# Selective-scan units whose product with B runs on GpSimd and whose decay lies in PSUM

## The chip, the cores and the metric

The kernel runs on one core of one Trainium2 chip. The metric is the device time of one execution in microseconds. The engines are called as in the profile: PE is TensorE, DVE is VectorE, ACT is ScalarE, POOL is GpSimd and SP is SyncE, which here issues nearly all DMAs.

## What is computed

Four layers work on an activation of 4 images x 1024 positions x 256 channels, in float32. The parts that matter here are the two selective scans, in layer 0 (512 inner channels, 64 states each) and in layer 3 (512 inner channels, 16 states each). In short:

```python
def step(h, inp):                                   # layer 0; layer 3 is alike
    xt, dtt, Bt, Ct = inp
    dA = jnp.exp(dtt[:, :, None] * A)               # the decay
    h = dA * h + (dtt * xt)[:, :, None] * Bt[:, None, :]
    y = jnp.einsum('bdn,bn->bd', h, Ct)
    return (h, y)
```

Around them layer 0 has a layer norm, a projection, a depthwise convolution, GELU and an output projection. Layer 1 is a residual block with a grouped convolution. Layer 2 is masked attention and a mixture of eight experts. Layer 3 has projections, the scan, a gate and another mixture of eight experts.

## The kernel before, in words

**Units.** A scan of one image is cut into units. One unit is a tile of 128 rows (channel times state) by 1024 steps of time: two channels of layer 0 or eight channels of layer 3. There are four images, so layer 0 has 4 x 256 units and layer 3 has 4 x 64, 1280 in all, numbered in the order of `SCANS`: (0,0), (0,1), (3,0), (0,2), (3,1), (0,3), (3,2), (3,3), where a pair is layer and image. Layer 3's units are thus 512 to 575, 832 to 895 and 1152 to 1279.

**What one unit takes.** `scans` writes the units as a software pipeline. In iteration k, in this order:

- `load(k + 4)`: SP loads the rows of dt, each repeated over the states, from DRAM into a tile `dA` (five buffers). That is two DMAs of 256 KB in layer 0 and eight of 64 KB in layer 3.
- `first(k + 1)`: two bf16 matmuls on PE spread dt times u over the states, from three bf16 parts, into a PSUM tile `ps_rep` (tag "x", two buffers).
- `decay(k + 2)`: ACT takes the exponential of the loaded tile in place, with a column of A as the scale.
- the mul: DVE multiplies `ps_rep` by the rows of B in PSUM. Then, after a `yield`, DVE runs `tensor_tensor_scan` with the decay from `dA` and the input from `ps_rep` into `h` (five buffers), and POOL multiplies `h` by the rows of C.
- `pair(k - 2)`, in every second iteration: PE sums two units over the states into `ps_y`, eight matmul records in the trace (four per unit). When a group of channels is full, ACT copies it out and SP stores it.

The scan of the next unit and the mul of the next unit follow on DVE in this order, so DVE alternates mul, scan, mul, scan. A `ps_rep` buffer comes free when the scan two units earlier ends.

**Side work.** Everything else inside `run` (the fronts of layer 0, then `middle(b)`, which holds layer 0's end, layers 1 and 2 and the front of layer 3, then `last(b)`) is a chain of Python generators. At each `yield` of `scans`, `run` may advance them by up to two steps. A planner, `Metered`, adds up a modelled cost for each engine; side work is admitted only as long as no engine's modelled clock is ahead of DVE's ("vector"), and no clock may lag DVE's by over 4 us:

```python
if max(clock.values()) > clock["vector"] + LEAD or self.advance() is None:
```

The order so found is the order of the instructions (the scheduler is set to manual). Where a scan needs something that side work hasn't produced, `need` advances the side work at once, with no scan between. For the last group of units, image 3 of layer 3, this happens between the scans of units 1210 and 1211. `last(3)` runs after all scans.

**The front's `steps`** compute dt and dt times u, store dt to DRAM, split dt times u in three bf16 parts and store these. The tile `x0`, 128 x 2048 float32 in SBUF, holds image 0 and is used by the first front only.

Most instructions are recorded through `Metered`'s helper, so the profile shows them at line 122; they are told apart by their tiles.

Of the kernel before, what the change touches and what calls it, by code (L numbers as in the profile page):

```python
# [16 lines left out]
P = 128  # L17
NB = 4
L = 1024
# [19 lines left out]
SORTS = 2  # L39
AHEAD = 12  # L40
LATEST = 5

LEAD, LAG, TICKS = 0.0, 4.0, 2
# [81 lines left out]
class Hybrid:  # L127
# [182 lines left out]
    def scan_setup(self, stage, psum, name, n):  # L310
# [16 lines left out]
        nc.vector.tensor_scalar(cols, cols, -1.0, None, ALU.mult)  # L327
        spread = pool.tile([3 * 32, 32 // G, P], BF16, name="spread_" + name)
        for s in range(3):
# [15 lines left out]
    def scans(self, mp, psum):  # L345
# [7 lines left out]
        nc = self.nc  # L353
        units = []
        for scan in SCANS:
            G = P // self.states[scan[0]]
# [2 lines left out]
                for d in range(DC) for c in range(2) for i in range(32 // G) for j in range(2)  # L359
            ]  # L360
        chunks, rows, waiting = {}, {}, []
        state = {}
        y = None

# [26 lines left out]
        def chunks_ahead(k):  # L391

            if k + AHEAD < len(units) and units[k + AHEAD][2:] == (0, 0, 0):
                waiting.append(k + AHEAD)
            while waiting:
                scan, d = units[waiting[0]][:2]
                if waiting[0] - k > LATEST and ("parts", *scan, d) not in self.ready:
                    break
                chunk(waiting.pop(0))

        def load(k):
            if k >= len(units):
                return
            scan, d, c, i, j = units[k]
            n = self.states[scan[0]]
            G = P // n
            a = mp.tile([P, L], F32, tag="dA", name="dA", bufs=5)
            for g in range(G):
                r = 64 * c + 32 * j + G * i + g
                nc.sync.dma_start(  # L410
                    a[g * n : (g + 1) * n, :],
                    self.mem["dt", *scan, d][r : r + 1, :].to_broadcast([n, L]),
                )
            state[k] = a

        def decay(k):
            if k >= len(units):
                return
            scan, d, c, i, j = units[k]
            G = P // self.states[scan[0]]  # L420
            col = (d * P + 64 * c + 32 * j) // G + i
            nc.scalar.activation(
                state[k], state[k], AF.Exp, scale=self.tables[scan[0]][0][:, col : col + 1]
            )

        def first(k):
            if k >= len(units):
                return
            scan, d, c, i, j = units[k]
            spread = self.tables[scan[0]][1]  # L430
            G = P // self.states[scan[0]]
            ps = psum.tile([P, L], F32, tag="x", name="ps_rep", bufs=2)
            for g in range(2):
                cols = slice(g * 512, (g + 1) * 512)
                nc.tensor.matmul(
                    ps[:, cols], lhsT=spread[:, i, :], rhs=chunks[scan, d][:, 2 * c + j, cols],
                    start=True, stop=True,
                )
            state[k] = (state[k], ps)
# [30 lines left out]
        for k in range(4):  # L470
            load(k)
        decay(0)
        decay(1)
        first(0)
        for k in range(len(units) + 4):
            chunks_ahead(k)
            load(k + 4)
            first(k + 1)
            decay(k + 2)
            if k < len(units):  # L480
                a, inp = state.pop(k)
                B, Cm = rows[units[k][0]]
                nc.vector.tensor_tensor(inp, inp, B, ALU.mult)
            yield
            if k < len(units):
                h = mp.tile([P, L], F32, tag="h", name="h", bufs=5)
                nc.vector.tensor_tensor_scan(h, a, inp, 0.0, ALU.mult, ALU.add)
                nc.gpsimd.tensor_tensor(h, h, Cm, ALU.mult)
                state[k] = h
            if k % 2 == 1 and 2 <= k < len(units) + 2:  # L490
                pair(k - 2)
            yield

    def need(self, scan, d):
# [26 lines left out]
    def run(self):  # L521

        self.done, self.ready = set(), set()
        self.todo, self.stage = list(STAGES), None
        nc, tc = self.nc, self.tc
        with tc.tile_pool(name="scan", bufs=1) as mp, tc.tile_pool(
            name="scps", bufs=1, space=PSUM
        ) as psum, tc.tile_pool(name="sdps", bufs=1, space=PSUM) as side, tc.manual_schedule():
            self.side_psum(side)
            self.mask_work, self.sorted = self.mask_prepare(), False  # L530
            clock = self.clock = dict.fromkeys(Metered.COST, 0.0)
            self.nc = Metered(nc, clock)
            for n, _ in enumerate(self.scans(mp, psum)):
                if n % 2:
                    next(self.mask_work, None)
                now = clock["vector"]
                for e in clock:
                    clock[e] = max(clock[e], now - LAG)
                for _ in range(TICKS):
                    if max(clock.values()) > clock["vector"] + LEAD or self.advance() is None:  # L540
                        break
            while self.advance() is not None:
                pass
            self.nc = nc
        assert not self.todo
# [7 lines left out]
    def steps(self, fp, key, w, src, chunks, bias, u):  # L553


        nc = self.nc
        for d in range(DC):
            self.keep(("dt", *key, d), [P, L])
            self.keep(("parts", *key, d), [3, P, L], BF16)
        got = {}  # L560

# [1194 lines left out]
```

## Time and profile before

| | |
|---|---|
| median of 3 runs | 6912.75 us (6912.15 to 6918.07) |
| the profiled execution | 6914.57 us, span 6912.9 us |
| PE busy | 5388.0 us, 78% |
| DVE busy | 5204.9 us, 75% |
| POOL busy | 3644.9 us, 53% |
| ACT busy | 3440.9 us, 50% |
| DMA queue of SP | 930.53 MB, 51.1% of 16 engines' span |
| granted PE clock, mean | 0.82 |

A row of the page's list of groups gives line, engine, operation, output and input tiles with their shape and count, then the busy time, the mean time of one in ns, and the idle time of the engine just before these instructions, with what ended it. A row of the timeline gives start, duration and engine. Busy shares are averages over stages that have different limits, so the stretches are looked at one by one.

### The profile page before, as it was taken

Reading aid. Unit: us, or ns where it says so; the run is one execution under the profiler, and the core shown is the slowest. Engines: PE = TensorE matmul, PEld = TensorE weight load, DVE = VectorE, ACT = ScalarE, POOL = GpSimd, SP = SyncE. Lnnn points to the kernel's source line nnn. Section 1 sums busy time; section 2 is a strip of 40 time slices with the busy share of each in tenths; the row PEclk is TensorE's granted clock in tenths of the full one; section 3 lists DMA queues with packets and bytes.
Section 4 is the critical chain, followed back from the end, with each engine's and each line's share of the span. In section 5 each row is a group of like instructions: output and inputs, shape, how many; then the busy total and the mean of one; then the engine's idle time right before and its main releaser. Section 6 shows DMA issues by size and latency. Waiting matters only on the chain. (4 is left out here: it accounts for less than half of the span.)

```text
span 6912.9 us, 66308 instructions
## 1 busy us (share of the span) xinstructions
PE 5388.0 (78%) x20516; PEld 2219.1 (32%) x20516; DVE 5204.9 (75%) x4477; ACT 3440.9 (50%) x4145; POOL 3644.9 (53%) x1801
## 2 busy tenths in 40 slices
PE   6558768678797567879689668798698678867979
PEld 3002212222342032234145322243253322523556
DVE  7778988877898986889889867898899840237411
ACT  2426667345476333457568334477386332244411
POOL 0876776755557654555856545557666530035200
PEclk8568768679898577989789779898698889877989
DMA  1556665654466665446656655456666630145321
GB/s 71 147 147 161 176 173 157 183 134 113 119 173 169 157 164 128 116 126 177 184 142 165 174 135 124 121 150 173 168 165 167 162 95 0 49 123 144 95 61 34
DMA packets 394239, 937.47 MB, mean 136 GB/s; under 512 B 83220, under 2 KB 165729, under 8 KB 392225
## 3 DMA queue, kind: packets, MB, share of 16 engines
q1 hardware_dynamic: 391696, 930.53, 51.1%
q8 instruction: 172, 2.82, 0.2%
q0 software_dynamic: 2128, 2.13, 0.2%
q14 instruction: 243, 1.98, 0.1%
HBM read 842.59 MB, written 93.95 MB: 135 GB/s over the span
## 5 line engine op out<-in xcount | busy, mean ns | idle before, releaser
L122 POOL TENSOR_TENSOR h<-h,rows 128x1024 f32<-128x1024 f32 x1280 | 3028.5, 2369 | 2002.5 <-DVE h L122 1620.7
L122 DVE TENSOR_TENSOR_SCAN h<-dA,ps_rep 128x1024 f32<-128x1024 f32 x1280 | 2924.6, 2285 | 209.8 <-issue 89.5
L122 DVE TENSOR_TENSOR ps_rep<-ps_rep,rows 128x1024 f32<-128x1024 f32 x1280 | 1553.3, 1213 | 336.3 <-PE ps_rep L122 313.8
L122 ACT ACTIVATE dA<-dA,A_L_conv_A_log 128x1024 f32<-128x1024 f32 x1024 | 1152.3, 1145 | 693.0 <-DMA dA<-dt 582.1
L122 PE MATMUL ps_rep<-S,spread_L_conv_A_log 96*128 96x512 bf16 x2048 | 755.7, 459 | 751.9 <-DVE h L122 696.0
L122 PE MATMUL ps_y<-h,collect_L_conv_A_log 128*32 128x512 f32 x4096 | 774.0, 750 | 104.3 <-POOL h L122 104.2
L122 ACT ACT_TABLE_LOAD x486 | 623.5, 1283 | 72.4 <-PE ps_h L122 49.9
L122 PEld LDWEIGHTS <-spread_L_conv_A_log 96*128 96x128 bf16 x2048 | 164.3, 103 | 1502.8 <-DVE h L122 1157.5
L122 PE MATMUL ps_h<-xTm,we 128*128 128x512 f32 x1280 | 605.7, 609 | 5.6 <-ACT h_m L122 4.5
L122 PE MATMUL ps_e<-we,h_m 128*128 128x256 f32 x2560 | 589.1, 382 | 6.8 <-ACT h_m L122 6.8
L122 ACT ACTIVATE p<-ps_sc 128x512 f32<-128x512 f32 x512 | 277.9, 594 | 588.7 <-PE ps_sc L122 558.6
L122 PEld LDWEIGHTS ps_e<-we,h_m 128*128 128x128 f32 x2560 | 483.2, 190 | 137.1 <-issue 46.7
L122 ACT ACTIVATE dA<-dA,A_L_attn_A_log 128x1024 f32<-128x1024 f32 x256 | 293.4, 1148 | 460.6 <-DMA dA<-dt 434.6
L122 PE MATMUL ps_at<-p,v 128*32 128x512 f32 x1024 | 361.6, 624 | 61.4 <-ACT p L122 53.3
L122 PE MATMUL ps_rep<-S,spread_L_attn_A_log 96*128 96x512 bf16 x512 | 188.8, 458 | 266.5 <-DVE h L122 220.9
L122 ACT ACTIVATE h_m<-ps_h,cols 128x512 f32<-128x512 f32 x320 | 217.0, 687 | 313.2 <-PE ps_h L122 310.4
L122 DVE SCALAR_TENSOR_TENSOR tb<-ps_e,cw,tb 128x256 f32<-128x256 f32 x448 | 192.6, 473 | 214.4 <-PE ps_e L122 214.4
L122 PEld LDWEIGHTS ps_h<-xTm,we 128*128 128x128 f32 x1280 | 242.5, 194 | 287.0 <-issue 238.7
L122 PE MATMUL ps_sc<-qT,kT 32*128 32x512 f32 x1024 | 301.8, 665 | 0.0
L122 PE MATMUL ps_at<-p,ones 128*32 128x512 f32 x1024 | 278.7, 624 | 0.0
L122 PE MATMUL ps_cv<-pad,diag 128*128 128x512 f32 x576 | 260.4, 593 | 0.0
L122 PEld LDWEIGHTS ps_y<-h,collect_L_conv_A_log 128*32 128x32 f32 x4096 | 101.3, 119 | 488.5 <-POOL h L122 240.3
(360 smaller groups left out, 5454.3 us busy)
## 6 DMA issues: line engine op xcount, KB each, us to landing
dA<-dt SPq DMA_DIRECT2D x2048, 256.0 KB
dA<-dt SPq DMA_DIRECT2D x2048, 64.0 KB
we<-in_L_ffn_W_dram SPq DMA_DIRECT2D x64, 512.0 KB
parts<-parts SPq DMA_DIRECT2D x64, 384.0 KB
S<-parts SPq DMA_DIRECT2D x96, 256.0 KB
dt<-sp_r SPq DMA_DIRECT2D x64, 256.0 KB
y<-yo SPq DMA_DIRECT2D x128, 128.0 KB
y_back<-y SPq DMA_DIRECT2D x64, 256.0 KB
```

The costliest lines, as they stand in the source:

```text
L122: return got(*args, **kw)
```

## The change

For some units, called *own* in the code, the input of the scan is made in another way. `steps` now also stores dt times u as float32 (`dtu`). `choose(k + 6)` decides, with a budget of POOL time that the planner leaves unused (`OWN`, 4.0 us each), whether unit k + 6 is own. If so, SP loads the rows of `dtu`, repeated over the states, into one half of `x0`. Two iterations ahead of the scan POOL multiplies this tile by the rows of B, in place. PE's two matmuls and DVE's mul are left out for this unit. Since the scan's input is then in SBUF, its decay goes to PSUM: the exponential reads the loaded `dA` and writes a tile `ps_dA`, from the same two buffers as `ps_rep`, one iteration later than before. For all units `h` has seven buffers instead of five, and `pair` sums units k - 5 and k - 4 instead of k - 3 and k - 2.

```diff
+OWN, EARLY = 4.0, 6
...
+        def spread(k, what, to):
...
+            for g in range(G):
+                r = 64 * c + 32 * j + G * i + g
+                nc.sync.dma_start(
+                    to[g * n : (g + 1) * n, :],
+                    self.mem[what, *scan, d][r : r + 1, :].to_broadcast([n, L]),
+                )
+
         def load(k):
...
+            state[k] = mp.tile([P, L], F32, tag="dA", name="dA", bufs=5)
+            spread(k, "dt", state[k])
+
+        def choose(k):
+            nonlocal spare
+            spare, self.unused = min(spare + self.unused, 1.5 * OWN), 0.0
+            if k >= len(units) or spare < OWN or units[k][:2] not in chunks:
+                return
+            if len(own) > 1 and k - EARLY <= list(own)[-2]:
+                return
+            spare -= OWN
+            i = 4 * (len(own) % 2)
+            own[k] = self.x0[:, i : i + 4, :].rearrange("p j c -> p (j c)")
+            spread(k, "dtu", own[k])
...
         def decay(k):
...
+            if k in own:
+                nc.gpsimd.tensor_tensor(own[k], own[k], rows[units[k][0]][0], ALU.mult)
+            else:
+                nc.scalar.activation(state[k], state[k], AF.Exp, scale=column(k))
 
         def first(k):
-            if k >= len(units):
+            if k >= len(units) or k in own:
                 return
...
-        for k in range(len(units) + 4):
+        for k in range(len(units) + 6):
             chunks_ahead(k)
+            choose(k + EARLY)
             load(k + 4)
             first(k + 1)
             decay(k + 2)
             if k < len(units):
                 a, inp = state.pop(k)
                 B, Cm = rows[units[k][0]]
-                nc.vector.tensor_tensor(inp, inp, B, ALU.mult)
+                if k not in own:
+                    nc.vector.tensor_tensor(inp, inp, B, ALU.mult)
+            if k + 1 in own:
+                ps = psum.tile([P, L], F32, tag="x", name="ps_dA", bufs=2)
+                nc.scalar.activation(ps, state[k + 1], AF.Exp, scale=column(k + 1))
+                state[k + 1] = ps, own[k + 1]
             yield
             if k < len(units):
-                h = mp.tile([P, L], F32, tag="h", name="h", bufs=5)
+                h = mp.tile([P, L], F32, tag="h", name="h", bufs=7)
                 nc.vector.tensor_tensor_scan(h, a, inp, 0.0, ALU.mult, ALU.add)
                 nc.gpsimd.tensor_tensor(h, h, Cm, ALU.mult)
                 state[k] = h
-            if k % 2 == 1 and 2 <= k < len(units) + 2:
-                pair(k - 2)
+            if k % 2 == 1 and 4 <= k < len(units) + 4:
+                pair(k - 4)
...
                 now = clock["vector"]
+                self.unused += max(0.0, now - LAG - clock["gpsimd"])
...
             self.keep(("dt", *key, d), [P, L])
+            self.keep(("dtu", *key, d), [P, L])
...
             nc.sync.dma_start(self.mem["dt", *key, d][:, g * 512 : (g + 1) * 512], r)
+            nc.sync.dma_start(self.mem["dtu", *key, d][:, g * 512 : (g + 1) * 512], x)
```

More of the change, by code (lines that the diff above doesn't have):

```diff
@@ L361, in scans @@
         chunks, rows, waiting = {}, {}, []
+        own, spare = {}, 0.0
         state = {}
@@ L399, in chunks_ahead @@
                 chunk(waiting.pop(0))
+        def spread(k, what, to):
+            scan, d, c, i, j = units[k]
+            n = self.states[scan[0]]
+            G = P // n
+            for g in range(G):
[4 more added lines that the diff above has]
+                )
         def load(k):
@@ L403, in load, with column @@
                 return
-            scan, d, c, i, j = units[k]
[L405 to L414, printed above, removed]
+            state[k] = mp.tile([P, L], F32, tag="dA", name="dA", bufs=5)
[11 more added lines that the diff above has]
+            spread(k, "dtu", own[k])
+        def column(k):
+            scan, d, c, i, j = units[k]
+            col = (d * P + 64 * c + 32 * j) // (P // self.states[scan[0]]) + i
+            return self.tables[scan[0]][0][:, col : col + 1]
         def decay(k):
@@ L418, in decay @@
                 return
[L419 to L424, printed above, removed]
+            if k in own:
+                nc.gpsimd.tensor_tensor(own[k], own[k], rows[units[k][0]][0], ALU.mult)
+            else:
+                nc.scalar.activation(state[k], state[k], AF.Exp, scale=column(k))
         def first(k):
-            if k >= len(units):
+            if k >= len(units) or k in own:
                 return
@@ L532, in run @@
             self.nc = Metered(nc, clock)
+            self.unused = 0.0
             for n, _ in enumerate(self.scans(mp, psum)):
```

## The prediction

> **What bounds the kernel now.** I read the page's costliest groups first, then where the scans of the 1280 units start in time, then the busy time by stretch, then waits and SP's timeline. A unit is one `tensor_tensor` (mul, with B) and one scan on DVE, one product with C on POOL, one exponential on ACT, two `ps_rep` matmuls and four `ps_y` matmuls on PE. From the page:
>
> ```profile
> L122 POOL TENSOR_TENSOR h<-h,rows 128x1024 f32<-128x1024 f32 x1280 | 3028.5, 2369 | 2002.5 <-DVE h L122 1620.7
> L122 DVE TENSOR_TENSOR_SCAN h<-dA,ps_rep 128x1024 f32<-128x1024 f32 x1280 | 2924.6, 2285 | 209.8 <-issue 89.5
> L122 DVE TENSOR_TENSOR ps_rep<-ps_rep,rows 128x1024 f32<-128x1024 f32 x1280 | 1553.3, 1213 | 336.3 <-PE ps_rep L122 313.8
> L122 ACT ACTIVATE dA<-dA,A_L_conv_A_log 128x1024 f32<-128x1024 f32 x1024 | 1152.3, 1145 | 693.0 <-DMA dA<-dt 582.1
> L122 PE MATMUL ps_rep<-S,spread_L_conv_A_log 96*128 96x512 bf16 x2048 | 755.7, 459 | 751.9 <-DVE h L122 696.0
> ```
>
> POOL works 2369 ns a unit and mostly waits for DVE (1620.7 us); PE and ACT wait for DVE and for loads. DVE works 3.5 us a unit. The timeline where DVE has nothing else shows the pace, 2312.17 to 2315.77, **3.60 us a unit**:
>
> ```profile
> 2312.17 1.21 DVE L122 TENSOR_TENSOR ps_rep<-ps_rep,rows 128x1024 f32<-128x1024 f32 x1
> ...
> 2313.57 2.29 DVE L122 TENSOR_TENSOR_SCAN h<-dA,ps_rep 128x1024 f32<-128x1024 f32 x1 [0.19 <-issue]
> ...
> 2315.77 1.21 DVE L122 TENSOR_TENSOR ps_rep<-ps_rep,rows 128x1024 f32<-128x1024 f32 x1
> ```
>
> By the start of each scan: unit 0 at 208 us, unit 512 at 2418, unit 1210 at 5663, unit 1211 at 6151, the last scan ends at 6480. Busy time in these stretches (PE, PEld, DVE, ACT, POOL, granted clock, DMA share, GB/s):
>
> ```profile
> 208.00:2418.00 2210.00, 1638.07 (x5841) 515.63 (x5840) 1934.95 (x1399) 1169.77 (x1427) 1499.26 (x757) 0.76 0.59 155
> 2418.00:5663.00 3245.00, 2597.24 (x10698) 1103.67 (x10700) 2723.36 (x2195) 1789.86 (x2032) 1862.81 (x871) 0.84 0.58 151
> 5663.00:6151.00 488.00, 408.14 (x1464) 178.62 (x1461) 75.69 (x184) 157.39 (x260) 45.17 (x36) 0.90 0.09 29
> 6151.00:6480.00 329.00, 232.23 (x858) 104.83 (x861) 266.04 (x216) 172.29 (x182) 190.95 (x93) 0.77 0.65 163
> 6480.00:6913.00 433.00, 389.18 (x1376) 262.39 (x1368) 60.56 (x154) 80.14 (x120) 17.06 (x13) 0.93 0.15 46
> ```
>
> Units 0 to 511 and 512 to 1210 are DVE's: busy 88% and 84%, with side work (convolutions, attention, experts) beside them. The third row is a **gap**: the scans of the last group need the rest of `middle(3)`, and for 488 us PE (84% busy) does that almost alone. In the fifth row no scan runs. So the change can gain in the first two rows, and what is left for the gap is paid at the side work's own pace.
>
> **The Trainium skill.** "GPSIMD Engine Reference", 3.1, gives a float32 `tensor_tensor` of 2048 columns 4497 ns on GpSimd and 2293 on DVE, 1.96 to 1; the trace has 2369 to 1213 for 1024, 1.95. "SBUF — State Buffer", Who interferes with whom: a DVE instruction with two SBUF inputs contends with a GpSimd one that reads SBUF, one with a single SBUF input doesn't. The trace agrees: `sp_x`, with two SBUF inputs, takes 1424 ns on average and 0.69 us in the gap at 6150 us, the scan 2225 to 2289 ns whatever POOL does. In the changed units the scan still has one input in PSUM (now the decay), so I leave it at 2285. "Perfetto Trace Analysis", DMA Instruction — HWDGE, says that the profiled time of an SP issue is the sequencer's, not the data's: so these times add up on SP.
>
> **The change part by part.** The order of the built programs shows 179 changed ("own") units: 75 below unit 512, 96 from 512 to 1210, 8 after; 138 in layer 0's scans, 41 in layer 3's.
>
> *DVE.* Each loses a mul: 1.21 us. 75 x 1.21 = -91 us; 96 x 1.21 = -116; 8 x 1.21 = -10. 358 matmuls go from PE (459 ns each), no gain where DVE sets the pace.
>
> *POOL.* 179 products more, 2369 ns each by the row of h: 424 us. In the first two stretches POOL was busy 1499 of 2210 and 1863 of 3245; with 75 and 96 more it comes to 1677 and 2090, below the time left. The product for unit k+2 stands between the C products of k-1 and k, and its scan starts some 7 us after scan k-1 ends; two POOL products need 4.7. So nothing, at most some 2 us at each bunched own unit (bounds 0 and 60 us; I take 0). Sums two units later give PE two units more before it waits for POOL, with 7 h buffers to cover it (0; at best -30: two such stalls of DVE, of 10.8 and 9.5 us, are seen around 3429 and 4893 us).
>
> *ACT.* The exponential goes to PSUM, 1145 ns as before, one iteration later. It waits for scan k-1 to end (same PSUM buffers as `ps_rep`), behind it are the decay of k+3 and side work. From there to its scan DVE has 3.5 us of work and it needs 1.15: nothing, provided the decay of k+2 ahead of it isn't waiting for its load. Bounds: -20 (DVE no longer waits for a late `ps_rep` in an own unit, 313.8 us over 1280 units x 179 = 44, half of it) and +40 (1 in 5 own units late by 1.15). I take 0.
>
> *DMA.* 604 loads and 64 stores more, 94 + 17 MB on 937: the share of the 16 engines goes from 51% to some 57%. Hidden in layer 0's scans, two issues a unit. Layer 3's units need eight issues each. From SP's timeline and its form table, where scans ran at 3.6 us a unit:
>
> ```profile
> 5423.95 26.11 SPq L410 DMA_DIRECT2D dA<-dt  x49
> L410 SPq DMA_DIRECT2D dA<-dt x49: 302/418/1388, 5424.0 to 5449.6; - x49
> ```
>
> 26.11 / 49 = 0.533 us each, 4.3 us for a unit's eight: **SP already runs at DVE's pace there**, living on five dA buffers and on stalls elsewhere (a layer 3 unit takes 5.3 us on average). Own units put eight more ahead of the next unit's load. For units 1152 to 1210 that is (59 + 12) x 8 = 568 issues, 244 us at 0.43 (the mean of these issues) or 303 at 0.533, where DVE would need some 227 (314 less 14 less the 73 below). So +17 to +76 there; 0 to +37 in units 832 to 895 (64 + 12, so 261 to 324 us, against 342 less 15 for the muls and some 40 for the 149 side rows of PE that move to later units); little elsewhere. I take **+45**, bounds 0 and 175 (all 328 issues at 0.533).
>
> *Side work moves.* The planner admits side work while no modelled clock is ahead of DVE's. An own unit advances DVE's by 1.27 us less, so less side work goes between scans. Order of side rows is unchanged on each compute engine; by unit 512 both programs have placed the same, but between scans 1210 and 1211 PE has 1122 side rows instead of 846 (leaving out a branch not taken), ACT 324 for 250, DVE 215 for 181. The 276 are what before had placed from unit 1166 on: the end of the convolution, norm, q, k, v, the shift, two of eight head pairs. *Taken from the scans*: units 1166 to 1210 took 5432.0 to 5663.5 = 231.5 us where 44 x 3.6 = 158.4 is DVE's own: **-73**. *Put into the gap*: head pairs run there at 136 us for four (5732 to 5868), so 68; q, k, v 29 (5487 to 5516); norm with transposes 20 (like 5879 to 5899); shift 42, between its 17 us of `ps_n` matmuls with the chain behind it and the 60 us that it took before; convolution's end 17. Sum **+176**, bounds 130 and 215.
>
> **Sum.** -91 - 116 - 10 - 73 + 176 + 45 = -69. The profiled run took 6914.57, with a span of 6912.9; it lies 1.8 us above the median 6912.75, from which I count: **6844 us**. Half of what DVE saves after unit 512 comes back in the gap.
>
> **Rivals.**
> *A larger gain.* The gap costs 130, SP hides its issues, late `ps_rep` and the later sums give 40 more: -69 - 46 - 45 - 40 = -200, 6713; with half of these 6779. For it: PE and DVE wait for each other, and own units loosen both. Against: SP's timeline. 0.22.
> *SP becomes the bound, slower.* In layer 3's scans (units 512 to 575, 832 to 895, 1152 on) each own unit's eight issues delay all loads behind them; if all 175 us show, -69 - 45 + 175 = +61, 6974. Decides from 128 of the 175. For it: the 4.3 us above. Against: these scans average 5.3 us a unit. 0.13.
> *It cancels.* Gap 215, SP 105: -69 + 39 + 60 = +30; half way, within 0.2%, 0.09.
> That the change doesn't act is excluded: 179 muls are missing in the built order.
>
> **Numbers.** The forecast, 6800 to 6890, has 0.56. About 14 us, 0.2%, is what a measurement of this kernel can tell from no change. Faster 0.78, same 0.09, slower 0.13. The range 6760 to 6930 leaves out the extremes of the first two rivals.
>
> **What would show it.** Right: DVE's mul x1101, 1336 us; POOL busy near 4070; unit 512 some 90 us earlier; unit 1210 some 235 earlier; the gap 640 to 690 us long; tail 433 as before; DVE's waits for dA loads up by some 45 us in layer 3's units. Wrong: scans of own units waiting for POOL or ACT by 0.5 us or more on average (179 x 0.5 = 90, all that is gained), a slower scan from PSUM, or a gap that stays at 490.

## The result: slower by 3.1%, and the profile after

The median is **7126.01 us** (7120.26 to 7141.0, 4 runs), against 6915.41 us for the kernel before in the same session: 1.0306 times, interval 1.0292 to 1.0321. Ratios below are to the kernel before in their own session in the same way; its median moved from 6915 to 6922 between sessions, so a few us between two kernels say little. The forecast was 6844. The profiled execution took 7141.0 us, with a span of 7139.3.

The costliest groups of the page of after (line, engine, operation, tiles, count; busy us, mean ns; idle time before and what ended it):

```profile
L125 POOL TENSOR_TENSOR h<-h,rows 128x1024 f32<-128x1024 f32 x1280 | 3018.6, 2363 | 1664.7 <-DVE h L125 1452.5
L125 DVE TENSOR_TENSOR_SCAN h<-dA,ps_rep 128x1024 f32<-128x1024 f32 x1101 | 2514.6, 2284 | 185.8 <-DMA dA<-dt 47.5
L125 DVE TENSOR_TENSOR ps_rep<-ps_rep,rows 128x1024 f32<-128x1024 f32 x1101 | 1334.6, 1212 | 289.8 <-PE ps_rep L125 271.9
...
L125 DVE TENSOR_TENSOR_SCAN h<-ps_dA,x 128x1024 f32<-128x1024 f32 x179 | 408.3, 2282 | 267.2 <-ACT ps_dA L125 235.4
...
L125 POOL TENSOR_TENSOR x<-x,rows 128x1024 f32<-128x1024 f32 x179 | 420.8, 2351 | 0.0
```

The 179 products have left DVE as forecast (x1101, 1334.6 us) and take 420.8 us on POOL. The own scans are no slower (2282 ns), but DVE sat idle for 267.2 us before them, 1.5 us each, 235.4 of it for the exponential into `ps_dA`. From the list of DVE's waits in after (total us, times, longest; the first lies mostly in the gap, 270.8 us of it):

```profile
DVE sums L125 <- ACT sums L125: 307.3, 16, 86.1
DVE ps_rep L125 <- PE ps_rep L125: 271.9, 157, 21.2
DVE h L125 <- ACT ps_dA L125: 236.0, 73, 12.5
...
DVE h L125 <- DMA dA<-dt: 62.7, 54, 19.0
```

The same five stretches as before, cut at the scans of units 0, 512, 1210, 1211 and at the last scan's end (length, then PE, PEld, DVE, ACT, POOL busy, granted clock, DMA share, GB/s):

```profile
223.60:2412.90 2189.30, 1589.49 (x5719) 499.89 (x5719) 1885.13 (x1341) 1156.48 (x1420) 1629.13 (x814) 0.76 0.67 174
2412.90:5703.30 3290.40, 2478.34 (x9989) 1036.82 (x9989) 2600.33 (x2047) 1709.31 (x1934) 2106.59 (x976) 0.82 0.65 167
5703.30:6353.40 650.10, 534.98 (x1944) 231.89 (x1944) 88.87 (x218) 204.79 (x338) 56.95 (x45) 0.89 0.09 30
6353.40:6705.50 352.10, 229.20 (x829) 106.15 (x829) 255.63 (x206) 163.30 (x175) 208.63 (x101) 0.72 0.62 166
6705.50:7139.30 433.80, 390.09 (x1394) 261.02 (x1393) 61.10 (x156) 81.13 (x121) 17.10 (x13) 0.94 0.16 48
```

The gap grew from 488 to 650.1 us, as forecast (640 to 690). But the scans from 512 to 1210, with 123 us less work on DVE (2723.36 to 2600.33), took 45 us *longer*, where the forecast had them 144 shorter (116 + 73 - 45); those below 512 took 21 us less with 50 less work. The question is thus where the time of the removed products went.

The kernels whose stretches are compared, in one table (us; the stretches are those of the profiled execution, worked out from the scans' starts in the trace; that execution lay up to 25 above the median):

| kernel | median | start | 0 to 511 | 512 to 1210 | gap | 1211 to end | tail |
|---|---|---|---|---|---|---|---|
| before | 6915 to 6922 | 208 | 2210 | 3246 | 488 | 329 | 433 |
| after | 7126 | 224 | 2189 | 3290 | 650 | 352 | 434 |
| e3: no own units | 6928 | 224 | 2211 | 3235 | 496 | 335 | 433 |
| e5: only order, later | 7061 | 224 | 2217 | 3225 | 627 | 331 | 440 |
| e15: only order, earlier | 7111 | 219 | 2293 | 3386 | 475 | 335 | 426 |
| e9: products gone, order of e3 | 6876 | 219 | 2176 | 3209 | 497 | 338 | 434 |
| e10: products gone, order moved | 6932 | 220 | 2159 | 3160 | 626 | 331 | 440 |
| e13: masks gone, order of e3 | 6816 | 220 | 2178 | 3146 | 495 | 341 | 434 |
| e14: both gone, order of e3 | 6762 | 220 | 2153 | 3126 | 492 | 336 | 433 |
| e1: `ps_dA` earlier | 7114 | 220 | 2173 | 3288 | 653 | 346 | 434 |
| e7: without loads of `dtu` | 6991 | 219 | 2188 | 3177 | 642 | 333 | 437 |
| e4: own, DVE's clock charged | 7185 | 219 | 2236 | 3379 | 562 | 354 | 430 |
| e12: own in layer 0 only | 6961 | 224 | 2194 | 3189 | 593 | 339 | 432 |
| e16: own, order of e3 | 7015 | 224 | 2216 | 3317 | 498 | 353 | 429 |
| e17: own in layer 0 only, order of e3 | 6917 | 220 | 2207 | 3238 | 497 | 336 | 435 |
| e18: own at 63 chosen units | 6895 | 221 | 2188 | 3218 | 497 | 339 | 435 |

### The profile page after: what moved, and what is told of

Its sections match the earlier page's. It is cut to its first block, busy times and chain, and to the rows that moved or that the text cites. A ratio compares the mean times of both kernels' runs of the same rounds, so it can differ in the third digit from the quotient of the medians.

```text
span 7139.3 us, 66309 instructions
## 1 busy us (share of the span) xinstructions
PE 5351.3 (75%) x20158; PEld 2192.2 (31%) x20158; DVE 5035.2 (71%) x4298; ACT 3386.2 (47%) x4113; POOL 4048.0 (57%) x1980
## 5 line engine op out<-in xcount | busy, mean ns | idle before, releaser
L125 DVE TENSOR_TENSOR_SCAN h<-dA,ps_rep 128x1024 f32<-128x1024 f32 x1101 | 2514.6, 2284 | 185.8 <-DMA dA<-dt 47.5
L125 DVE TENSOR_TENSOR ps_rep<-ps_rep,rows 128x1024 f32<-128x1024 f32 x1101 | 1334.6, 1212 | 289.8 <-PE ps_rep L125 271.9
L125 ACT ACTIVATE dA<-dA,A_L_conv_A_log 128x1024 f32<-128x1024 f32 x886 | 1001.3, 1145 | 654.0 <-DMA dA<-dt 564.1
L125 PE MATMUL ps_rep<-S,spread_L_conv_A_log 96*128 96x512 bf16 x1772 | 671.2, 469 | 852.6 <-DVE h L125 819.7
L125 PE MATMUL ps_y<-h,collect_L_conv_A_log 128*32 128x512 f32 x4096 | 735.8, 754 | 36.7 <-POOL h L125 36.6
L125 DVE TENSOR_TENSOR_SCAN h<-ps_dA,x 128x1024 f32<-128x1024 f32 x179 | 408.3, 2282 | 267.2 <-ACT ps_dA L125 235.4
L125 ACT ACTIVATE dA<-dA,A_L_attn_A_log 128x1024 f32<-128x1024 f32 x215 | 246.5, 1148 | 545.6 <-DMA dA<-dt 473.8
L125 PE MATMUL ps_at<-p,v 128*32 128x512 f32 x1024 | 385.8, 642 | 78.9 <-ACT p L125 73.4
L125 PE MATMUL ps_rep<-S,spread_L_attn_A_log 96*128 96x512 bf16 x430 | 163.5, 470 | 355.6 <-DVE h L125 324.4
L125 POOL TENSOR_TENSOR x<-x,rows 128x1024 f32<-128x1024 f32 x179 | 420.8, 2351 | 0.0
```

The costliest lines, as they stand in the source:

```text
L125: return got(*args, **kw)
```

## The experiments

Theory A at the start: the own scans' wait for ACT (267 us) ate the gain. Rival B: the loads of `dtu` on SP's queue. Rival C: the side work's new order. Rival D: DVE's time was not worth what the forecast took. CHOSEN below is the list of the 179 own units, fixed, so that kernels can be compared unit by unit. "Order" is the order of instructions that the planner makes, and a change "at a fixed order" is charged in the planner as what it replaces.

### The start and the order of the side work: e3, e5, e15

*e3* keeps everything of after, but no unit becomes own:

```diff
-OWN, EARLY = 4.0, 6
+OWN, EARLY = 1.0e9, 6
```

> No own unit is chosen; what remains of the change is the store of dt u (64 DMAs), seven h buffers and the sums two units later. All theories: as before within 20 us (6895 to 6935), gap near 490; if the later sums or the stores were the cause, 7000 or more.

Measured: 6927.9 us (20 runs), 1.0013 (1.0005 to 1.0021). Seven `h` buffers and later sums bring no gain; the 64 stores of `dtu` go with a first scan that starts 11 to 17 us later in all kernels that have them. e3 is the base for what follows.

*e5* has no own units either; only the planner's DVE clock is held back by a product in the 179 units, which moves side work as in after:

```diff
                 if k not in own:
                     nc.vector.tensor_tensor(inp, inp, B, ALU.mult)
+                if k in CHOSEN:
+                    self.clock["vector"] -= 0.06 + 1.18e-3 * L
```

> No own unit, but the planner's clock of DVE is held back by one mul in each of the 179 units that the change had chosen, so side work moves as in the changed kernel (1097 side rows of PE in the gap; 846 before, 1122 after). Theory C (the moved side work is a cost of its own): the gap near 640 us, the scans before it 75 us shorter, so +80 to +100 against e3, about 7015. If the move is neutral: 6928 within 20.

Measured: 7061.08, 1.0204 (1.0182 to 1.0226), 133 us over e3. The gap of e5, in the same columns as above:

```profile
5665.30:6292.40 627.10, 510.99 (x1906) 222.82 (x1905) 88.92 (x217) 202.60 (x335) 56.85 (x45) 0.90 0.10 31
```

The gap takes 131 us more, and the scans before it give back only 10 (3235 to 3225). On balance side work beside scans was nearly free; in the gap it is paid in full. The prediction had put the relief in units 1166 to 1210. First e3, then e5, for these units:

```profile
5449.40:5670.10 220.70, 159.82 (x686) 63.13 (x689) 161.19 (x121) 90.75 (x117) 118.31 (x57) 0.78 0.53 135
```

```profile
5445.20:5665.30 220.10, 157.59 (x638) 82.54 (x637) 176.09 (x143) 101.26 (x100) 113.97 (x53) 0.86 0.62 161
```

They took as long as before the move. The attention that stood there went to the gap, and side work that had stood beside earlier units moved in: 160 records of the experts' `ps_e` matmuls stand there in e5, none in e3.

*e15* is the opposite:

```diff
                 if k in CHOSEN:
-                    self.clock["vector"] -= 0.06 + 1.18e-3 * L
+                    self.clock["vector"] += 0.06 + 1.18e-3 * L
```

> No own units (as e3), only the order changed: the planner's VectorE clock is advanced by one product (1.27 us) more in each of the 179 units, the opposite of e5, so that side work is issued earlier beside the scans: 820 PE rows are left in the gap between the layers, against 876 in e3. If side work beside scans is nearly free and its price is paid in the gap (e5: +131 in the gap for 221 rows more, 0.59 us a row): gap -33, scans +0 to +5, about 6895 to 6900. If the order of before is already where both cancel: within 10 us of e3 (6928). If side work crowds scans as in e4: slower, up to +60.

Measured: 7110.94, 1.0274 (1.0254 to 1.0294), 183 us *over* e3. The gap shrank by 21 us and the scans grew by 81 and 151. Of the theories in the expectation only the last, that side work crowds the scans, had the direction, and at a third of the size. DVE's wait for `ps_rep` rose from 292.3 us in e3 to

```profile
DVE ps_rep L138 <- PE ps_rep L138: 378.1, 218, 10.7
```

which fits side matmuls standing ahead of the units' own. The rise is 86 of the 183 us; the rest isn't taken apart. The order of before costs time when it is moved either way.

### What a product is worth: e9, e10, e13, e14

*e9* leaves the product out in the 179 units, while the planner charges it, so the order is that of e3:

```diff
-                if k not in own:
+                if k not in CHOSEN:
                     nc.vector.tensor_tensor(inp, inp, B, ALU.mult)
+                else:
+                    self.clock["vector"] += 0.06 + 1.18e-3 * L
```

> As e3 (no own units, no loads of dt u, nothing on POOL or ACT in another place), but the mul of DVE is left out in the 179 units (the scan reads dt u without B from PSUM), and the planner is charged as if it were there, so that the order is that of e3 but for these instructions. It measures what 217 us less of DVE are worth by themselves. If DVE sets the pace, as the prediction had it: 6928 - 217 = 6711, by 180 at the least. Theory F (side work on PE and ACT sets the pace in step with DVE): 6928 - 60 to 110, so about 6840.

Measured: 6876.04, 0.9941 (0.9925 to 0.9958). **217 us less work on DVE are worth 52 us**, 0.24 for 1. Nothing takes the products' place here. The 358 matmuls, which the change takes off PE as well, stay in e9; what they are worth alone wasn't measured.

*e10* is e9 without the charge, so that the planner moves the side work:

```diff
-                else:
-                    self.clock["vector"] += 0.06 + 1.18e-3 * L
```

> As e9, but the planner sees the missing mul, so side work moves as in the changed kernel. The prediction's sum without its +45 for SP: 6928 - 217 - 73 + 176 = 6814. Theory C with the cost of the move as e5 measured it (+133): e9 + 133 if the two terms add up, about 6970; in the changed kernel the rest, 7126 less this, is then what loads, ACT's order and POOL add.

Measured: 6932.09, 1.0013 (1.0 to 1.0025). The gap grows by 129 us and the scans give back only 67 more: all of the gain is gone. Even with no work in the products' place on POOL, ACT or SP, leaving out these 179 did not win under this planner.

*e13* asks what paces the scans instead. It leaves out the attention's mask matmuls, again with the order of e3:

```diff
-                    start=True, stop=False,
+                    start=True, stop=True,
...
-            for i in range(2):
-                nc.tensor.matmul(
-                    two[i], lhsT=self.onesb[rows[i], :], rhs=mT[rows[i], c, qs],
-                    start=False, stop=False,
-                )
-            for i in range(2):
-                nc.tensor.matmul(
-                    two[i], lhsT=self.identb, rhs=maskT[:, kb, qs], start=False, stop=True
-                )
+            self.clock["tensor"] += 3 * 0.46e-3 * 512
```

> No own units (as e3), and the 1024 mask products of the attention heads (ps_sc<-mT,onesb 100.9 us and ps_sc<-maskT,identb 160 us busy in the profile of before, 261 us of PE) are left out, so the attention is unmasked; the planner charges them as if they were there, so the order is that of e3. About 49 us of them lie in the gap between layers, the rest beside scans. If PE sets the pace of the stretches in which side work runs: -49 in the gap and -100 to -200 beside the scans, 6680 to 6780. If PE's time is worth what DVE's was in e9 (0.21 to 0.24): -49 in the gap and about -45 beside the scans, some 6835. If VectorE alone set the pace: only the gap, about 6880.

Measured: 6816.46, 0.9856 (0.9835 to 0.9876), 111 us below e3: the scans gave 34 and 89. The gap gave nothing, against 49 expected (see the last section). Blocks of 32 units show where. Units 320 to 351 have attention beside them, units 1088 to 1119 have not. First e3, then e13, then e9, in the columns of the stretches:

```profile
1608.90:1761.30 152.40, 130.71 (x678) 38.15 (x688) 122.32 (x83) 74.82 (x109) 83.00 (x39) 0.93 0.44 112
5116.30:5242.00 125.70, 122.09 (x507) 65.98 (x506) 119.20 (x91) 107.58 (x100) 76.39 (x33) 1.00 0.60 163
```

```profile
1592.20:1728.90 136.70, 114.15 (x560) 30.34 (x560) 120.11 (x83) 73.80 (x107) 82.88 (x39) 0.90 0.48 125
5005.90:5131.60 125.70, 122.09 (x507) 65.99 (x506) 119.22 (x90) 107.32 (x101) 76.31 (x33) 1.00 0.61 163
```

```profile
1584.90:1738.10 153.20, 131.83 (x690) 38.58 (x696) 116.95 (x77) 76.05 (x110) 84.06 (x39) 0.93 0.43 112
5054.30:5175.80 121.50, 118.54 (x494) 64.05 (x493) 114.61 (x87) 104.78 (x98) 76.27 (x33) 1.00 0.64 168
```

The attention block follows PE: 16.6 us less PE work is 15.7 us less time (152.4 to 136.7), while DVE's 5.4 us less is worth nothing (153.2). In the other block 4.6 us less DVE work is 4.2 less time (125.7 to 121.5). But PE is busy 97% there, and its busy time fell by 3.6, with 13 records fewer, so this block alone doesn't tell DVE from PE. Units 448 to 479, with PE busy 58%, do. First e3, then e9:

```profile
2195.60:2320.10 124.50, 72.48 (x216) 14.32 (x216) 118.05 (x74) 57.43 (x65) 100.05 (x51) 0.59 0.65 181
```

```profile
2163.70:2283.10 119.40, 71.65 (x218) 14.43 (x218) 113.39 (x70) 57.28 (x65) 100.75 (x52) 0.61 0.68 189
```

Here 4.7 us less on DVE is 5.1 less time. DVE was busy 80%, 95% and 95% of these three blocks in e3; an average of 84 or 88% over the stretch hid that. Yet a high busy share isn't enough. In units 640 to 671, with no attention, DVE is busy 97% in e3 and PE 90%:

```profile
3093.60:3233.60 140.00, 126.64 (x519) 68.95 (x518) 135.27 (x143) 112.21 (x111) 74.67 (x33) 0.95 0.61 163
```

```profile
3052.10:3191.20 139.10, 126.92 (x520) 69.27 (x519) 128.75 (x135) 112.68 (x111) 74.53 (x33) 0.95 0.61 164
```

In e9 (second line) 6.5 us less on DVE is worth 0.9.

Over all scans the 179 products divide in three (e3 less e9, by the scans' starts):

| units | products | full price | gained |
|---|---|---|---|
| layer 0, blocks with attention beside them | 34 | 41 | 7 |
| layer 0, the rest | 104 | 126 | 66 |
| layer 3 | 41 | 50 | -16 |

So attention is only one part of it. In layer 3's units loads come late already in e3. In units 512 to 543, which take 163 us, ACT waits for them for 72.1:

```profile
ACT dA L125 <- DMA dA<-dt: 72.1, 18, 26.0
```

What else holds layer 0's rest isn't taken apart.

*e14* takes both out, with the edits of e9 and e13.

> e13 with e9's edit too: the product with B is left out in the 179 units (as in e9) and the attention is unmasked; order of e3. If VectorE and PE each hold the other back in turn (a step waits for PE in one place and for VectorE in the next), the two together gain clearly more than the sum of e9 (-52) and e13. If they bound different stretches of the program, just the sum. If a third thing (ScalarE, or the order itself) sets the pace, less than the sum.

Measured: 6761.97, 0.9767 (0.9746 to 0.9789), 166 us below e3, against 52 + 111 = 163 for the two alone. That is just the sum, within the few us by which medians move, as it would be if they pace different places.

### ACT, the loads and POOL: e1, e11, e7, e2, e8, e6

*e1* issues the exponential into `ps_dA` ahead of the decay of unit k + 2, in place of after it:

```diff
             first(k + 1)
+            if k + 1 in own:
+                ps = psum.tile([P, L], F32, tag="x", name="ps_dA", bufs=2)
+                nc.scalar.activation(ps, state[k + 1], AF.Exp, scale=column(k + 1))
+                state[k + 1] = ps, own[k + 1]
             decay(k + 2)
```

> Same 179 own units; only the order on ACT differs: the exponential into PSUM for unit k+1 is emitted ahead of the decay of unit k+2 instead of behind it. Theory A (the own scan waits because its exponential stands behind another unit's decay, and so behind that unit's load): the waits of own scans fall from 267 us to about 75 (59 in layer 0's units, 15 in layer 3's, worked out from the changed kernel's trace by taking that decay out of the way), so the time falls from 7126 to about 6935. Theory B (SP's eight issues for each own unit of layer 3 delay all loads behind them, whatever the order on ACT): layer 3's 152 us of waits stay, as waits for loads; only layer 0's fall, so about 7070. Theory C (side work pushed into the gap) expects the gap at 650 us in either case.

Measured: 7113.53, 1.028 (1.0263 to 1.0297). DVE's waits in e1:

```profile
DVE ps_rep L125 <- PE ps_rep L125: 359.3, 186, 21.4
...
DVE h L125 <- ACT ps_dA L125: 79.3, 45, 4.1
```

157 us of the wait for `ps_dA` are gone, and 87 came up at once as a wait for `ps_rep`; 13 us were gained. **Theory A falls**: this wait is where DVE stood, and taking it away gained little.

*e7* leaves the 604 loads of `dtu` out.

```diff
-            spread(k, "dtu", own[k])
```

> The changed kernel without the 604 loads of dt u: the product takes what lies in x0, so the scans of own units have other input data. Theory E (the loads burden SP and the DMA engines and delay the other loads): layer 3's own scans wait 30 us in all instead of 152, and the time falls by 120 or more, to 7000. Theory D: it falls by 0 to 60, as layer 0's waits and the ties of ACT stay.

Measured: 6990.5, 1.0104 (1.0081 to 1.0126): 136 us less than after. From the scans' starts, 19 + 39 + 35 + 19 = 112 of the profiled difference of 143 lie in layer 3's units (512 to 575, 832 to 895, 1152 to 1210, after 1211). But the loads aren't all. Without them the own units still cost 58 us over e10, where the products are simply gone. By the scans' starts e7 is 58 longer than e10 in layer 0's units, 16 longer in the gap and 10 shorter in layer 3's units. The two orders differ a little, so this is not the own units' price alone.

*e11* joins the edits of e1 and e7.

> The changed kernel without the loads of dt u (as e7, 6990) and with the exponential into PSUM ahead of the other unit's decay (as e1). Own scans in e7 waited 194 us. If ACT's order costs these: 6990 - 120 = 6870. If, as with the loads present (e1: only 13 us less for 174 us less of own waits), the wait only moves to the next unit: 6990 - 10 to - 30.

Measured: 6989.76, 1.0113 (1.0091 to 1.0134), no more than e7 alone. A second time most of the wait for `ps_dA` went (173.0 us in e7, 66.6 here), and nothing was gained.

*e2* loads a layer 3 unit's eight rows in one DMA of 512 KB, dt and `dtu` alike:

```diff
+            r = 64 * c + 32 * j + G * i
+            if n < 64:
+                nc.sync.dma_start(
+                    to,
+                    self.mem[what, *scan, d][r : r + G, :].unsqueeze(1).to_broadcast([G, n, L]),
+                )
+                return
```

> The changed kernel, but in layer 3 one DMA of 512 KB loads a unit's rows (of dt and of dt u) instead of eight of 64 KB; the order on ACT is unchanged. SP then issues one instruction instead of eight. Theory B: layer 3's 152 us of waits of own scans vanish, and layer 3's units get faster beyond that, so 6970 or less. Theory A without B (loads land late, not for their issue but for the transfer): layer 3's waits stay above 100 us, 7100. The waits of layer 0's own scans, 115 us, stay in both.

Measured: 7099.4, 1.0255 (1.0234 to 1.0275), 27 us less than after. SP issues once where it issued eight times. But where ACT waits for a layer 3 load, it gets it some 11.5 us after the issue ends, against 2.1 for the eight small ones (medians): one cost for another.

*e8* leaves POOL's 179 products out and still charges them.

```diff
-                nc.gpsimd.tensor_tensor(own[k], own[k], rows[units[k][0]][0], ALU.mult)
+                self.clock["gpsimd"] += 0.06 + 2.3e-3 * L
```

> The changed kernel without POOL's 179 products (the scan takes dt u without B; the planner is charged for the product all the same, so that the order stays). If POOL's load delays the C products and through them PE: the time falls by 50 or more. Theories D and E: within 20 of 7126.

Measured: 7121.65, 1.0295 (1.0274 to 1.0316): 4 us. POOL was free, as forecast.

*e6* keeps the decay of own units in SBUF, so that their scan reads two SBUF inputs:

```diff
-            else:
+            if True:
                 nc.scalar.activation(state[k], state[k], AF.Exp, scale=column(k))
...
             if k + 1 in own:
-                ps = psum.tile([P, L], F32, tag="x", name="ps_dA", bufs=2)
-                nc.scalar.activation(ps, state[k + 1], AF.Exp, scale=column(k + 1))
-                state[k + 1] = ps, own[k + 1]
+                state[k + 1] = state[k + 1], own[k + 1]
```

> The changed kernel with the decay of own units in SBUF, in the place and order of the others (no PSUM tile, no wait of ACT for a scan); the scan of an own unit then reads both inputs from SBUF. Theory D (the exponential into PSUM ties ACT to the scan two units back; ACT's side work queues behind it and holds up PE and then DVE): own scans wait for no decay, ACT's side work flows as before, so 7126 - 200 = 6925, less what two SBUF inputs cost: between 0 and 1.2 us for each own scan (POOL is busy 57%), 0 to 215, so 6925 to 7090, with the own scan's mean above 2400 ns. Theory E (loads): stays at 7100 or more with the own scan's mean below 2400 ns.

Measured: 7188.07, 1.0387 (1.0365 to 1.041), 62 us over after. The groups of e6, shapes kept apart:

```profile
L125 POOL TENSOR_TENSOR h<-h,rows 128x1024 f32<-128x1024 f32 x1280 | 3234.7, 2535 | 1485.2 <-DVE h L125 1267.3 <-PE ps_rep L125 61.7 <-DVEq L1219 18.7
L125 DVE TENSOR_TENSOR_SCAN h<-dA,ps_rep 128x1024 f32<-128x1024 f32 x1101 | 2515.2, 2284 | 235.8 <-DMA dA<-dt 67.4 <-ACT dA L125 59.9 <-issue 25.0
L125 DVE TENSOR_TENSOR_SCAN h<-dA,x 128x1024 f32<-128x1024 f32 x179 | 522.5, 2920 | 32.0 <-DMA dA<-dt 18.1 <-POOL x L125 7.8 <-ACT dA L125 3.9
```

The own scan takes 2920 ns in place of 2282, and POOL's product 2535 in place of 2363. The Trainium skill ("SBUF — State Buffer", Who interferes with whom) says that a DVE instruction with two SBUF inputs contends with a GpSimd instruction that reads SBUF. The trace agrees and gives a price: 179 x 0.64 = 114 us on DVE. The decay in PSUM earns its place, though the wait before these scans is only 32.0 us without it.

### The order against the own units: e4, e12, e16, e17

*e4* has the 179 own units, and the planner's DVE clock advances by a product in each.

```diff
+                else:
+                    self.clock["vector"] += 0.06 + 1.18e-3 * L
```

> The same 179 own units, listed by number, but the planner's clock of DVE is advanced in an own unit as if the mul were still there, so that side work isn't held back: the gap has 1011 side rows of PE instead of 1122 (846 before). Theory C: the gap falls from 650 to about 585 us, the scans before it slow down by some 0.4 of this, so the time falls by 30 to 45, to about 7085. Theory A alone: the gap is worth nothing net, 7126 give or take 15.

Measured: 7185.06, 1.038 (1.0362 to 1.0397). The gap is 88 us shorter than after's, and the scans 47 and 89 longer. The order is still not e3's: the planner also charges POOL, ACT and PE otherwise in an own unit.

*e12* allows own units in layer 0 only. They are chosen anew (140, of which 69 are not in CHOSEN), so it doesn't compare with the others unit by unit:

```diff
-            if k >= len(units) or spare < OWN or units[k][:2] not in chunks:
+            if k >= len(units) or units[k][0][0] or spare < OWN or units[k][:2] not in chunks:
```

> The changed kernel with own units in layer 0's scans alone (140 instead of 179; 376 eight-fold issues fewer on SP in layer 3, so that SP there is as before). Theory B (eight issues for each own unit of layer 3): what e7 saved in layer 3's units comes back, 113 us, with some 30 us more from the gap (1045 side rows of PE instead of 1122), so about 6985. If the loads cost by their bytes, as much in layer 0: 7080.

Measured: 6960.96, 1.0054 (1.0033 to 1.0075), with a gap of 593.

*e16* charges an own unit on every engine as any other, so that the order is e3's:

```diff
+            if k in own:
+                self.clock["tensor"] += 2 * 0.46e-3 * 512
...
+                self.clock["gpsimd"] -= 0.06 + 2.3e-3 * L
+                self.clock["scalar"] += 0.18 + 0.95e-3 * L
...
+                self.clock["scalar"] -= 0.18 + 0.95e-3 * L
...
+                else:
+                    self.clock["vector"] += 0.06 + 1.18e-3 * L
```

> The change with all its 179 own units, but the planner charges an own unit on every engine exactly as any other (product with B on VectorE, two matmuls on PE, decay on ScalarE at its old place, nothing for GpSimd), so that side work keeps the order of e3: 875 PE rows in the gap between the layers against 876. It separates what the order costs from what the own units cost. Gap about 497. By the sum of the other runs: e9 (6876, the products gone at this order) plus 58 (the machinery of own units, e7 over e10) plus 136 (their loads, after over e7) = 7070. If the own units are harmless as long as the order stays: 6876 to 6900. If the order is what costs, and the loads as such do not: 6900 to 6950.

*e17* is e16 with own units in layer 0 only (138 of CHOSEN):

```diff
-            if k not in CHOSEN:
+            if k not in CHOSEN or units[k][0][0]:
                 return
```

> As e16, own units in layer 0's scans alone (138, with two loads each instead of eight): e12 without its move of side work. e12 took 6961 with 1045 PE rows in the gap; here 876, gap about 497. If the order's price comes back: 6961 less some 40 (e10 over e9 scaled by 138 of 179) to less 96 (the gap's shrinking) = 6865 to 6920. If the own units' own cost is what e12 showed: within 10 us of 6961.

Measured: e16 7015.05, 1.0137 (1.0122 to 1.0153); e17 6917.35, 0.9997 (0.9989 to 1.0006). Three differences make up the account. After less e16 is **+111, the order** (the gap alone 152, the scans give 53 back). e16 less e9 is **+139, the own units themselves**. e16 less e17 is +98: the net price of **layer 3's 41 own units**. e17 is 11 us below e3, so layer 0's 138 gain a little. They don't come free either. By the scans' starts, layer 0's units gain 73 us in e9 and 22 in e17: what takes the products' place costs some 50 there.

How a layer 3 own unit loses is seen at unit 856 in e16. SP's queue (start, duration, operation), then ACT, then DVE:

```profile
4042.01 2.70 SPq L402 DMA_DIRECT2D S<-parts  x3
4044.81 3.95 SPq L424 DMA_DIRECT2D x<-dtu  x8
4048.99 14.18 SPq L424 DMA_DIRECT2D dA<-dt  x31
```

```profile
4058.17 1.15 ACT L138 ACTIVATE dA<-dA,A_L_attn_A_log 128x1024 f32<-128x1024 f32 x1 [12.69 <-DMA dA<-dt]
4059.23 1.10 ACT L138 ACTIVATE ps_dA<-dA,A_L_attn_A_log 128x1024 f32<-128x1024 f32 x1
```

```profile
4060.43 2.29 DVE L138 TENSOR_TENSOR_SCAN h<-ps_dA,x 128x1024 f32<-128x1024 f32 x1 [8.70 <-ACT ps_dA L138]
```

SP issues eight loads of `dtu` for unit 858 (3.95 us), and the loads of dt queue behind them, first unit 856's, then unit 857's. The decay of unit 857 waits 12.69 us for its load. The exponential of unit 856 stands behind it on ACT, and DVE waits 8.70 us for it. Unit 856's own load was late too, but it was ahead by one unit's eight issues (an estimate of 3.7 us, 8 of the 31 in 14.18), so the delay is due in part to SP and in part to the order on ACT. "PSUM — Partial Sum Buffer", Engine vs sequencer instructions, in the Trainium skill, calls ScalarE's queue strict FIFO, and this trace agrees. Over all layer 3 units the first load is issued 9.0 us (median) after its buffer comes free in e16, 5.4 in e3.

### A version that beats both: e18

*e18* is e17 with e1's edit, and with own units only in 15 of layer 0's blocks of 32, those in which e9 gained over 2.5 us (one more, at 288, has much attention beside it and is left out). That makes 63 units:

```diff
+GOOD = (64, 128, 192, 256, 352, 384, 448, 480, 704, 736, 768, 800, 1024, 1088, 1120)
...
-            if k not in CHOSEN or units[k][0][0]:
+            if k not in CHOSEN or k // 32 * 32 not in GOOD:
                 return
```

> As e17, but own only in the blocks of 32 units in which e9 gained (no attention beside them; 63 own units, all in layer 0), and the exponential into PSUM is issued ahead of the next unit's decay, as in e1. e9's gain in these blocks was 61 us; machinery and loads at the rate of the other runs (58 x 63/179 and some 13) take 33 back: 6928 - 61 + 33 = 6900, just faster than before (0.997). If the products were worth that gain only because nothing took their place (a wait of the scan on ScalarE or on the load does now): 6930 or more, the same as before or slower.

Measured: **6894.93**, 0.9963 (0.995 to 0.9977): faster than before by 0.37%, with a third of the own units. By the scans' starts these 15 blocks are 44 us shorter than in e3. How much of that the choice of units brings and how much e1's edit wasn't separated. In its groups, DVE waits 23.6 us in all before the own scans, 0.4 each in place of 1.5:

```profile
L139 DVE TENSOR_TENSOR_SCAN h<-ps_dA,x 128x1024 f32<-128x1024 f32 x63 | 143.2, 2275 | 23.6 <-ACT ps_dA L139 10.3 <-DMA dA<-dt 3.4 <-PE ps_rep L139 3.4
```

## Why the prediction was wrong

By medians, the way from before to after is: before 6917; e3 +11 (3 to 15 by its interval); products out, e9, -52; own units, e16, +139; order, after, +111; in all 7126. These steps are taken in one order; the order's price alone is 133 without own units (e5) and 56 with the products gone (e10 less e9), so it depends on what else is there.

- **DVE's products, -217 forecast, -52 measured (e9). This step failed most**, by 165 us. It said "Units 0 to 511 and 512 to 1210 are DVE's: busy 88% and 84%", and priced each product at its full 1.21 us. In e9 layer 0's 34 products with attention beside them gave 7 of 41 us, because PE paces those blocks (e13). Layer 3's 41 gave none of 50, in units where ACT waits for loads as it is, and the other 104 gave 66 of 126. "358 matmuls go from PE, no gain where DVE sets the pace" rests on the same premise; they stay in e9. With layer 0's gone as well (e17), the blocks with attention still gain only 1 us. The counts of own units were also off: 56 below unit 512 and 115 from 512 to 1210, not 75 and 96.
- **Loads, +45 forecast within 0 to 175.** The mechanism was right and its place too, layer 3's units; its size wasn't. Without the loads after is 136 us faster (e7), and layer 3's own units cost 98 at a fixed order (e16 less e17). SP was not "at DVE's pace" on average: its issues fill 268 of 370 us in units 512 to 575 of e16. A late load delays ACT and then DVE (unit 856). What the loads alone cost at that order wasn't run. Rival 2 named this; with products worth 52 in place of 217 it needed far less than its 128 us to decide.
- **ACT, 0 forecast within -20 to +40. Wrong for the waits; the price is in part open.** The own scans waited 267 us, over the 0.5 us each that the prediction named as a sign against it. Its proviso, "provided the decay of k+2 ahead of it isn't waiting for its load", is what failed: with the exponential ahead of that decay, 157 us of the wait went (e1; unit 856 shows one). Taking the wait away gained only 13, though, and nothing beside e7 (e11). Own units without their loads still cost 58 us over e10, by the scans' starts in layer 0's units. Which part of them, or of the order, does that stays open; POOL's product costs 4 (e8).
- **POOL, 0 forecast**: 4 us (e8), right. **The scan from PSUM** at 2285: 2282, right; e6 shows what the other way would cost.
- **Order, -73 and +176, so +103 forecast**: measured +111 (after less e16), of it +152 in the gap and -53 in the scans. The sum came out right by luck. The gap was a little too dear, and the -73 was reasoned wrongly: the prediction took it from units 1166 to 1210, as if nothing would fill the room. In e5 they take 220.1 us against 220.7 in e3, in after 244.7, because side work of earlier units moves in. The relief in after less e16 lies elsewhere, 71 in layer 3's units, of which layer 0's give 17 back. By itself the move relieved units 512 to 1210 by 10 us only (e5).
- **Stores of `dtu` and later sums, 0 forecast**: +11 (e3). The sums' upside of 30 didn't show.

The four errors, 165 + 94 (own units, 139 against 45) + 8 + 11, make the 278 us between a forecast of -69 and +209.

## What to carry to other kernels

Before an engine's time is priced at full value, cut its busy share into pieces as short as the side work beside it, and leave work out at a fixed order: here 217 us of an engine that was 84 to 88% busy were worth 52. The test counts more than the share: in one block the engine was 97% busy, and 6.5 us less of its work gave 0.9. When work moves out of a stretch, ask what moves in. Where a planner decides the order by modelled costs, a change of one operation changes the order too; charge the new operation as the old one first, and measure the two apart. A load added to a shared queue is paid by what stands behind it, so move work only where the engine relieved sets the pace and the queue has room (as in e18).

## What was not expected of the hardware

Leaving matmuls out made the others slower. The gap of e3, then of e13, in the columns of the stretches:

```profile
5670.10:6166.30 496.20, 409.80 (x1507) 178.64 (x1517) 78.97 (x184) 163.26 (x270) 46.85 (x37) 0.92 0.10 31
```

```profile
5544.00:6038.70 494.70, 400.37 (x1316) 173.99 (x1313) 78.98 (x184) 163.12 (x269) 46.97 (x37) 0.85 0.10 32
```

191 fewer matmul records took only 9 us off PE's busy time, the granted clock fell from 0.92 to 0.85, and the gap stayed. Over the whole span the product of q and k took 701 ns on average in e13 against 661 in e3. The Trainium skill ("TensorE: Matmul & The Clock Gate", What's actually happening) has a clock that is set by how busy PE has been, which these numbers agree with; how much of the missing 49 us the clock explains, and how much the chain from PE to ACT and back, isn't settled.

The exponential takes 1108 ns into PSUM and 1145 into SBUF (units of layer 0, after), a small gain that the forecast left out.
